# Pipelined routing head: one tile between producer and consumer, scatters in pairs, a shorter sort before the last slots

## The chip, the core and the metric

The kernel runs on one core of a Trainium2 chip, as one launch. The metric is the device time of a run in microseconds (us); lower is better. Before the change the median of three runs is 5019.25 us (5018.96 to 5019.48). The core's engines run beside each other, each through its own queue in order: TensorE (PE, with its weight loads shown apart as PEld), VectorE (DVE), ScalarE (ACT), GpSimd (POOL), and SyncE (SP), which here only issues DMAs.

## The reference

The program is one "macaron" block on x of shape (8, 1024, 512), that is, 8192 tokens of 512 numbers: half a feed-forward, attention, half a feed-forward.

```python
x = x + 0.5 * ffn(layernorm(x))
x = x + attention(layernorm(x))
x = x + 0.5 * ffn(layernorm(x))
```

The feed-forward is a mixture of 32 experts with one expert per token and a capacity of C = 320 tokens per expert:

```python
logits = xt @ w_router                      # 8192 x 32
probs = softmax(logits); top1 = argmax(probs); gate = probs[top1]
pos = cumsum(onehot(top1), axis=0)[token, top1] - 1
accepted = pos < C
slot = where(accepted, top1 * C + pos, E * C)
buf[slot] = xt                              # E x C x 512
y = (silu(buf @ w_gate) * (buf @ w_up)) @ w_down
out = xt + where(accepted, y[slot] * gate, 0)
```

So the place of a token among those of its expert depends on all tokens before it. The attention has 16 heads of 32, with rotary embedding, and doesn't change here.

## The kernel before

Each feed-forward has two stages. A **head** finds the expert, the gate and the slot of every token and scatters (token number, gate) into a table in DRAM, one row of 8 bytes per token. The **experts' stage** (`experts`, L443) reads this table back, gathers the tokens of one expert after another from DRAM by index, computes, and scatters the results.

In the first half of the program the head is `front` (L287). Its loop (L343) goes over 64 tiles of 128 tokens. The tiles form nine groups: 4 tiles, seven times 8, and 4. In iteration i it

- normalizes tile i on ACT (`h`, L134), transposes it on PE in four matmuls (`tp`, L156), and copies the transposed tile i - 1 from PSUM to SBUF (`xT`, L355; on ACT, every eighth on DVE),
- takes the mean and variance of tile i + 10 on DVE (`stats`, L113 and L114),
- moves every open piece of work one step on (`advance`). Such a piece is a Python generator: each `yield` in it ends its step for this iteration; what the `yield` says (WAIT, PE, DVE) is not used in this loop.

Three kinds of generators are open. `normalizing` (L116) makes the scales of a group: a sum on DVE (L124), a power on POOL (`rstd`, L125), and one step later their products on DVE (`nmr`, L127). `routers` (L176) makes the logits of four tiles: eight passes of PE for `pl` (L184), a copy on ACT (`parts`, L189), a step later eight for `lp` (L194) and a copy on ACT (`lg`, L197). `route` (L200) takes a whole group: maxima on DVE, an exponential on ACT (L227), one-hot columns and their running counts (`oh`, `run`, L232 to L238), PE products that count the tokens before each one (`pp`, L242 and L246), the position (L250 to L258), then 14 small DVE operations that turn it into the slot, and at last the group's scatters, one per tile, all in one step, as indirect DMAs of POOL (L279). A group's `route` begins only when that of the group before has ended, since the running counts go on from it.

The order on PE, ACT, DVE and POOL is the order of these Python calls (`manual_schedule`). Only SP's order is left to the compiler of the program. So an instruction that waits holds up all that is behind it on its engine.

When the loop and its open work are done, `sorted` (L373) ranks the experts by their token counts. It gives a matrix that puts the table's columns in this order, `order` (which expert is first, read by SP to find its weights) and `arm` (which of three copies of the experts' loop fits the counts). In it some 36 DVE operations and four matmul pairs depend on each other.

`experts` then loads the table (`slots`, L478), folds its last columns (L483), multiplies it by the matrix (`pt`, L486), turns the result into indices (`come`, L488), starts the gathers of the first two experts (L555), loads the first expert's weights with three DMAs of 1 MB (L546), and clears two buffers `a` on POOL (L482), which the experts' activations are written to.

In the second half of the program the head's work is spread through the attention (`finished`, L1276), group by group of four tiles, with its own scheduler (`step`, `product`); `sorted` follows after the last group (L885).

Of the kernel before, what the change touches and what calls it, by code (L numbers as in the profile page):

```python
# [14 lines left out]
I32 = mybir.dt.int32  # L15
# [35 lines left out]
class Block:  # L51
# [58 lines left out]

    def stats(self, pool, mv, x):
        st = pool.tile([P, 6], F32, tag="bnst", bufs=4, name="st")
        self.nc.vector.bn_stats(st, x)  # L113
        self.nc.vector.bn_aggr(mv, st)  # L114
# [61 lines left out]
    def routers(self, xT, lg, pool, psum, tag, bufs):  # L176
# [6 lines left out]
        for k in range(KD):  # L183
            nc.tensor.matmul(  # L184
                pl[k * E : (k + 1) * E, :], self.w_router[:, k, :], xT[:, k, :],
                start=True, stop=True,
            )
        parts = pool.tile([P, 4 * P], F32, tag="parts", bufs=bufs, name="parts")
# [4 lines left out]
        for j in range(4):  # L193
            nc.tensor.matmul(  # L194
                lp[:, j, :], parts[:, j * P : (j + 1) * P], self.fold, start=True, stop=True
            )
        self.copy(lg, lp)  # L197
        yield WAIT, 1

    def route(self, t0, lg, pool, psum, tag, carry, table, spare=None):  # L200
# [8 lines left out]
        def wide(name):  # L209
            return pool.tile([P, G, E], F32, tag=name, bufs=1, name=name)  # L210
# [26 lines left out]
        for j in range(G):  # L237
            nc.vector.tensor_tensor(run[:, j + 1, :], run[:, j, :], oh[:, j, :], ALU.add)  # L238
        yield WAIT, 1
# [9 lines left out]
        )  # L249
        nc.vector.tensor_tensor(lg, pp, oh, ALU.mult)  # L250
# [5 lines left out]
        pos, ok, s, u = narrow("pos"), narrow("ok"), narrow("s"), narrow("u")  # L256
        slot = narrow("slot", I32)
        nc.vector.tensor_reduce(pos, lg, AX.X, ALU.add)  # L258
        yield DVE, 2.0

        nc.vector.scalar_tensor_tensor(s, m, float(-P), pos, ALU.mult, ALU.add)
        for i in range(1, self.NB):
            nc.vector.tensor_scalar(
                u, pos, float(i * P), float((E - 1) * P), ALU.is_ge, ALU.mult
            )
            nc.vector.tensor_tensor(s, s, u, ALU.add)

        nc.vector.tensor_scalar(ok, pos, float(C), None, ALU.is_lt)
        nc.vector.tensor_scalar(s, s, float(E * P - self.NS), None, ALU.add)
        nc.vector.tensor_tensor(s, s, token, ALU.subtract)  # L270
        nc.vector.tensor_tensor(s, s, ok, ALU.mult)
        nc.vector.tensor_tensor(s, s, token, ALU.add)
        nc.vector.tensor_scalar(slot, s, float(self.NS), None, ALU.add)
        if spare is not None:
            nc.vector.tensor_scalar(ok, pos, float(C), None, ALU.is_ge)
            nc.vector.scalar_tensor_tensor(u, token, float(-self.T), ok, ALU.add, ALU.mult)
            nc.vector.tensor_scalar(spare[:, t0 : t0 + G], u, float(self.T), None, ALU.add)
        for j in range(G):
            nc.gpsimd.indirect_dma_start(  # L279
# [7 lines left out]
    def front(self, pool, psum, x, rest, spare, carry, table):  # L287
# [12 lines left out]
        def load(t):  # L300
            xs[t // 4] = xq = pool.tile([P, 4, D], F32, tag="xq", bufs=6, name="xq")
# [13 lines left out]
        def routed(g):  # L315

            while state.next < g:
                yield
            state.carry = yield from self.route(
                starts[g], lgs[g], pool, psum, "lp", state.carry, table, spare  # L320
            )
            state.next += 1

        def products(t):
# [3 lines left out]
                xTs.pop(t // 4), lg[:, at : at + 4, :], pool, psum, "lp", bufs=2  # L328
# [11 lines left out]
        ahead, late = G + 2, None  # L340
        load(0)
        load(4)
        for i in range(-ahead, NT + 2):  # L343
            if 0 <= i < NT:
# [3 lines left out]
                h = pool.tile([P, D], F32, tag="h", bufs=4, name="h")  # L348
                self.normalize(h, tile_of(i), (r, n, None, None), i)
                if i % 4 == 0:  # L350
                    xTs[i // 4] = pool.tile([P, KD, 4 * P], F32, tag="xT", bufs=3, name="xT")
                tp = self.turned(psum, "tp", h)
            if late:
                to, from_, j = late
                (nc.vector.tensor_copy if j % G == G - 1 else nc.scalar.copy)(to, from_)  # L355
                if j % 4 == 3:
                    work.append(products(j))
            late = None
            if 0 <= i < NT:
                late = xTs[i // 4][:, :, i % 4 * P : (i % 4 + 1) * P], tp, i  # L360
# [10 lines left out]
        return state.carry  # L371

    def sorted(self, pool, psum, tag, counts):  # L373
# [3 lines left out]
        nc, E, NB = self.nc, self.E, self.NB  # L377
        R = NB * E
        wide = pool.tile([P, NB, E], F32, name="wide")
        for i in range(NB):  # L380
            nc.vector.tensor_copy(wide[:, i, :], counts)


        keys, mine = pool.tile([P, E], F32, name="keys"), pool.tile([R, E], F32, name="mine")
        many = pool.tile([R, P], F32, name="many")
        pc = psum.tile([P, E], F32, tag=tag, name="pc")
        nc.tensor.matmul(pc, self.ones, counts, start=True, stop=True)
        nc.vector.scalar_tensor_tensor(keys, pc, float(E), self.rev[:, 0, :], ALU.mult, ALU.add)
        pr = psum.tile([R, P], F32, tag=tag, name="pr")
        nc.tensor.matmul(  # L390
            pr, wide.rearrange("p b e -> p (b e)"), self.ones, start=True, stop=True
        )
        nc.vector.tensor_copy(many, pr)
        nc.vector.tensor_scalar(mine, many[:, 0:E], float(E), None, ALU.mult)
        nc.vector.tensor_tensor(mine, mine, self.rev[:R, 0, :], ALU.add)

        own = pool.tile([R, E], F32, name="own")
        for i in range(NB):
            at = slice(i * E, (i + 1) * E)
            nc.vector.tensor_copy(own[at, :], self.ident[at, at])  # L400
        key, rank = pool.tile([R, 1], F32, name="key"), pool.tile([R, 1], F32, name="rank")
        nc.vector.tensor_tensor(mine, mine, own, ALU.mult)
        nc.vector.tensor_reduce(key, mine, AX.X, ALU.add)
        nc.vector.tensor_scalar(mine, keys[:R, :], key, None, ALU.is_gt)
        nc.vector.tensor_reduce(rank, mine, AX.X, ALU.add)

        place = pool.tile([R, E], F32, name="place")
        nc.vector.tensor_scalar(place, self.rev[:R, 0, :], -1.0, float(E), ALU.mult, ALU.add)
        nc.vector.tensor_scalar(place, place, rank, None, ALU.is_equal)
        matrix = pool.tile([R, R], F32, name="matrix")  # L410
        nc.vector.memset(matrix, 0.0)
        for i in range(NB):
            at = slice(i * E, (i + 1) * E)
            nc.vector.tensor_copy(matrix[at, at], place[at, :])

        cols = pool.tile([E, 2, P], F32, name="cols")
        nc.vector.tensor_tensor(mine[0:E, :], self.rev[0:E, 0, :], self.ident[0:E, 0:E], ALU.mult)
        nc.vector.tensor_reduce(rank[0:E, :], mine[0:E, :], AX.X, ALU.add)
        nc.vector.tensor_scalar(rank[0:E, :], rank[0:E, :], -1.0, float(E), ALU.mult, ALU.add)
        nc.vector.tensor_copy(cols[:, 0, :], rank[0:E, :].to_broadcast([E, P]))  # L420
# [996 lines left out]
```

## Time and profile before

| what | value |
|---|---|
| median of the runs | 5019.25 us |
| profiled execution: its own time | 5020.19 us |
| profiled execution: span from first to last instruction | 5018.3 us |
| PE busy | 4682.0 us (93% of the span) |
| DVE busy | 2869.2 us (57%) |
| ACT busy | 2927.2 us (58%) |
| POOL busy | 790.2 us (16%) |
| mean granted PE clock | 0.962 |

Busy time by stretch, in us, with the granted clock of PE as a share of full speed:

| stretch (us) | PE | DVE | ACT | POOL | PE clock |
|---|---|---|---|---|---|
| 80 to 120 | 19.53 | 15.56 | 13.16 | 16.86 | 0.59 |
| 120 to 160 | 22.18 | 21.52 | 15.69 | 9.43 | 0.54 |
| 200 to 240 | 16.71 | 18.57 | 9.52 | 22.37 | 0.63 |
| 240 to 280 | 12.36 | 17.37 | 2.98 | 12.68 | 0.51 |
| 300 to 320 | 20.00 | 7.93 | 3.54 | 6.80 | 1.00 |

The first experts' stage begins its matmuls at 274.57 us and ends near 1085, the attention lasts to about 4160, and the second experts' stage begins its matmuls at 4196.53.

How to read it: a row of the timeline or of a group names the line, the engine, the operation and, as out<-in, the tiles; in brackets stand the idle time before it and what ended that. In the chain of waits each row is a start in us, a length in us, and the engine, tile and line that carried the time. A row of waits gives who waited for whom: us in total, times, and the longest. A PE that is busy at half clock does half the work, so the clock stands beside it.

### The profile page before, as it was taken

What the parts mean: (1) busy time and instruction counts of PE and PEld (TensorE: products, weight loads), DVE (VectorE), ACT (ScalarE), POOL (GpSimd) and SP (SyncE); (2) the same over time, 40 slices, a digit from 0 to 9 for tenths busy, and PEclk for the clock granted to TensorE, in tenths of its full rate; (3) what the DMA queues carried; (4) which work ended last, traced back from release to release, by engine and by line L of the source; (5) the groups of instructions that cost most, each with busy time, mean ns of one, the idle gap of its engine ahead of it and who ended that gap; (6) DMA issues with size and microseconds to landing.
All of it is one profiled execution on the core that took longest, in us unless ns stands there. A gap on an engine that the chain in (4) does not pass through costs nothing.

```text
span 5018.3 us, 68972 instructions
## 1 busy us (share of the span) xinstructions
PE 4682.0 (93%) x24572; PEld 2150.1 (43%) x24572; DVE 2869.2 (57%) x5678; ACT 2927.2 (58%) x5851; POOL 790.2 (16%) x773
## 2 busy tenths in 40 slices
PE   5489999978899999999999999999999876999998
PEld 3256666753223333333333333333333224666676
DVE  5433333335766777777777777777777744333332
ACT  4311112115998888888888888888888841111111
POOL 2322333211000000100010110110110002222221
PEclk6689999988999999999999999999999997999999
DMA  3055556641111211221211212212211124445553
GB/s 128 10 200 179 183 185 197 207 158 32 35 34 34 72 58 48 71 57 53 71 54 54 72 46 64 66 45 66 60 41 56 47 68 153 157 163 168 165 186 132
DMA packets 290538, 486.07 MB, mean 97 GB/s; under 512 B 47847, under 2 KB 83121, under 8 KB 290176
## 3 DMA queue, kind: packets, MB, share of 16 engines
q1 hardware_dynamic: 255328, 404.36, 25.6%
q0 software_dynamic: 34560, 76.93, 5.0%
q8 instruction: 197, 3.23, 0.3%
q14 instruction: 165, 1.35, 0.1%
q10 hardware_dynamic: 288, 0.20, 0.0%
HBM read 380.11 MB, written 89.72 MB: 94 GB/s over the span
## 4 chain that ended last, share of the span: by engine, by line
PE 80%; DVE 8%; ACT 5%; issue 3%; POOL 1%; DMA 1%; SPq 1%; DVEq 0%; POOLq 0%; ACTq 0%
PE sa L1153 13%; PE gp L638 9%; PE up L638 9%; PE pq L1058 8%; PE yp L677 8%; PE po L1235 8%; PE sb L1133 5%; PE px L1261 4%; PE pv L1103 4%; PE sb L1160 3%; ACT junk L1172 2%; DVE nm L1168 2%; PE tp L156 2%; PE tp L626 2%; PE yp L685 1%
## 5 line engine op out<-in xcount | busy, mean ns | idle before, releaser
L1168 DVE TENSOR_REDUCE nm<-sa 128x2 f32<-128x1024 f32 x1024 | 1249.4, 1221 | 650.3 <-PE sa L1153 388.0
L1172 ACT ACTIVATE junk<-sa,nm 128x512 f32<-128x512 f32 x2048 | 1408.2, 688 | 268.1 <-DVE nm L1168 194.5
L1153 PE MATMUL sa<-k,q 32*128 32x512 f32 x4096 | 1149.8, 645 | 20.9 <-ACT junk L1172 11.4
L1165 ACT ACTIVATE pr<-sb 128x1024 f32<-128x1024 f32 x1024 | 1041.3, 1018 | 99.3 <-PE sb L1160 95.0
L1160 PE MATMUL sb<-q,k 32*128 32x512 f32 x4096 | 1062.7, 602 | 0.0
L643 ACT ACTIVATE sg<-gp 128x320 f32<-128x320 f32 (+3 forms) x256 | 102.9, 402 | 1229.0 <-PE gp L638 1092.9
L1083 POOL TENSOR_TENSOR raw<-raw,cs 128x512 f32<-128x512 f32 x128 | 165.1, 1289 | 2474.5 <-DMA rot<-raw 1746.0
L1235 PE MATMUL po<-pr,v 128*32 128x512 f32 x4096 | 548.8, 607 | 0.1
L638 PE MATMUL gp<-bT,wg 128*128 128x320 f32 (+3 forms) x2048 | 533.3, 404 | 2.8 <-issue 2.0
L638 PE MATMUL up<-bT,wu 128*128 128x320 f32 (+3 forms) x2048 | 525.1, 399 | 0.0
L1058 PE MATMUL pq<-hT,wqk 128*128 128x512 f32 x1024 | 510.6, 623 | 6.6 <-DVE raw L1073 3.6
L677 PE MATMUL yp<-wd,a 128*128 128x512 f32 x1024 | 453.7, 596 | 0.0
L638 PEld LDWEIGHTS gp<-bT,wg 128*128 128x128 f32 x2048 | 387.8, 191 | 118.9 <-issue 31.6
L1133 PE MATMUL sb<-mrow,ones 3*128 3x512 bf16 x2048 | 393.4, 385 | 43.6 <-ACT pr L1165 38.9
L638 PEld LDWEIGHTS up<-bT,wu 128*128 128x128 f32 x2048 | 389.5, 190 | 94.7 <-issue 0.8
L662 DVE TENSOR_TENSOR a<-sg,up 128x320 f32<-128x320 f32 (+3 forms) x256 | 114.2, 446 | 550.7 <-PE up L638 510.5
L1133 PEld LDWEIGHTS <-ones 3*128 3x128 bf16 x2048 | 100.6, 91 | 711.9 <-issue 670.5
L1172 ACT ACTIVATION_READ_ACCUMULATOR junk<-sa,nm 128x1 f32 x2048 | 397.8, 194 | 0.0
L1160 PEld LDWEIGHTS sb<-q,k 32*128 32x128 f32 x4096 | 360.0, 184 | 0.1
L1153 PEld LDWEIGHTS sa<-k,q 32*128 32x128 f32 x4096 | 305.2, 184 | 86.2 <-ACT pr L1165 36.0
L1058 PEld LDWEIGHTS pq<-hT,wqk 128*128 128x128 f32 x1024 | 176.1, 191 | 325.3 <-issue 227.4
L681 DVE SCALAR_TENSOR_TENSOR ys<-yp,at,x 128x512 f32<-128x512 f32 x128 | 96.1, 751 | 369.0 <-PE yp L677 369.0
(179 smaller groups left out, 4341.0 us busy)
## 6 DMA issues: line engine op xcount, KB each, us to landing
wg<-in_w_gate SPq DMA_DIRECT2D x64, 1024.0 KB
wu<-in_w_up SPq DMA_DIRECT2D x64, 1024.0 KB
wd<-in_w_down SPq DMA_DIRECT2D x64, 1024.0 KB
rot<-raw SPq DMA_DIRECT2D x1024, 32.0 KB
xq<-in_x SPq DMA_DIRECT2D x16, 1024.0 KB
all<-in_x SPq DMA_DIRECT2D x32, 512.0 KB
xt<-first_rows SPq DMA_DIRECT2D x64, 256.0 KB
xr<-first_rows SPq DMA_DIRECT2D x64, 256.0 KB
```

The costliest lines, as they stand in the source:

```text
L638: nc.tensor.matmul(acc, w[:, k, f * P : (f + 1) * P], to.bT[:, k, 0:width], start=(k == 0), stop=(k == s.KD - 1),)
L677: nc.tensor.matmul(yp, a[:, f, i * P : (i + 1) * P], wd[:, f, :], start=(f == 0), stop=(f == KF - 1),)
L1058: nc.tensor.matmul(acc, w[:, which, k, :], self.hT[b, n][:, k, :], start=(k == 0), stop=(k == KD - 1),)
L1103: nc.tensor.matmul(acc, hT[:, k, at : at + P], self.w_vo[:, k, :], start=(k == 0), stop=(k == KD - 1),)
L1133: nc.tensor.matmul(sb[:, h, :], self.ones16[at : at + 3, :], row[at : at + 3, :], start=True, stop=False,)
L1153: nc.tensor.matmul(sa[:, h, :], qa[at, (g * 4 + j) * P : (g * 4 + j + 1) * P], ka[at, m * 512 : (m + 1) * 512], start=True, stop=True,)
L1160: nc.tensor.matmul(sb[:, h, :], k[at, t * P : (t + 1) * P], q[at, n * 512 : (n + 1) * 512], start=False, stop=True,)
L1165: nc.scalar.activation(pr, sb, AF.Exp)
L1168: nc.vector.tensor_reduce(nm[:, m, j, pair : pair + 2], sa, AX.X, ALU.max, negate=True)
L1172: nc.scalar.activation(self.junk, sa[:, h - pair, :], AF.Exp, bias=nm[:, m, j, h : h + 1], accum_out=se[:, m, j, h : h + 1],)
L1235: nc.tensor.matmul(self.po[at : at + HD, :], self.v[b][t][:, c * P + at : c * P + at + HD], prs[h // 2 * 2][:, h % 2, :], start=(t == 0), ...
L1261: nc.tensor.matmul(acc, self.oT[b, c, half][:, j * P : (j + 1) * P], self.w_vo[:, c, :], start=False, stop=(c == KD - 1),)
```

## The change

It has six parts.

1. In `front` the h of a tile is made two iterations ahead of its transposition, the statistics 12 iterations ahead instead of 10, and the copy of the transposed tile is issued ahead of the next transposition. A seventh buffer `xq` is there for the rows.
2. With `apart`, `routers` and `route` end their step between a PE product and the copy or product that reads it from PSUM. The scatters of a group are issued two in a step. A group's `route` may begin its counts as soon as the group before has its own (`counted`).
3. The slots take 9 DVE operations instead of 14, from three constants made at the start (`past`, `away`, `beyond`).
4. `sorted` takes the counts as soon as the last group has them. Six DVE operations make the matrix from constants; `rest` makes `order` and `arm` on one partition instead of 128. `route` runs it ahead of the last group's slots.
5. In `experts` the first expert's weights are issued on SP ahead of the table's load, and `come` is made straight from PSUM.
6. The buffers `a` are made and cleared once, at the start; the attention keeps its cosines and sines in them.

The diff, cut to its core:

```diff
 def constants(self, pool, w_router):
...
+        for t, add in (
+            (self.past, NS), (self.away, NS - E * P), (self.beyond, -self.T)
+        ):
+            nc.vector.tensor_scalar(t, self.token, float(add), None, ALU.add)
...
+        nc.gpsimd.memset(self.columns, -1.0)
+        for i in range(NB):
+            at = slice(i * E, (i + 1) * E)
+            nc.vector.tensor_copy(self.own[at, :], self.ident[at, at])
+            nc.vector.tensor_scalar(
+                self.columns[at, at], self.rev[at, 0, :], -1.0, float(E), ALU.mult, ALU.add
+            )
...
+        self.acts = [pool.tile([P, self.KF, self.C], F32, name=f"a{i}") for i in range(2)]
+        for t in self.acts:
+            nc.gpsimd.memset(t, 0.0)

 def routers(self, xT, lg, pool, psum, tag, bufs, apart=False):
...
+        if apart:
+            yield WAIT, 1
         parts = pool.tile([P, 4 * P], F32, tag="parts", bufs=bufs, name="parts")
         self.copy(parts, pl)
...
+        if apart:
+            yield WAIT, 1
         self.copy(lg, lp)

 def route(..., spare=None, apart=False, counted=None):
...
+        order = counted and counted(run[:, G, :])
         yield WAIT, 1
         yield PE, 1.2
         pp = psum.tile([P, G, E], F32, tag=tag, name="pp")
...
+        if apart:
+            yield WAIT, 1
         nc.vector.tensor_tensor(lg, pp, oh, ALU.mult)
...
+        if order:
+            at_once(order)
+
+        tokens = slice(t0, t0 + G)
+        nc.vector.tensor_scalar(u, pos, float(P), None, ALU.is_ge)
+        for i in range(2, self.NB):
+            nc.vector.scalar_tensor_tensor(u, pos, float(i * P), u, ALU.is_ge, ALU.add)
         nc.vector.scalar_tensor_tensor(s, m, float(-P), pos, ALU.mult, ALU.add)
+        nc.vector.scalar_tensor_tensor(s, u, float((E - 1) * P), s, ALU.mult, ALU.add)
+
+        nc.vector.tensor_tensor(s, s, self.away[:, tokens], ALU.subtract)
+        nc.vector.scalar_tensor_tensor(s, pos, float(C), s, ALU.is_lt, ALU.mult)
+        nc.vector.tensor_tensor(slot, s, self.past[:, tokens], ALU.add)
...
         for j in range(G):
+            if apart and j % 2 == 0:
+                yield WAIT, 1
             nc.gpsimd.indirect_dma_start(

 def front(...):
-            xs[t // 4] = xq = pool.tile([P, 4, D], F32, tag="xq", bufs=6, name="xq")
+            xs[t // 4] = xq = pool.tile([P, 4, D], F32, tag="xq", bufs=7, name="xq")
...
+            def counted(counts):
+                state.carry = counts
+                state.next += 1
+                if state.next == len(sizes):
+                    return ranked(counts)
...
-        ahead, late = G + 2, None
+        ahead, soon, late, hs = G + 4, 2, None, {}
...
         for i in range(-ahead, NT + 2):
+            if 0 <= (t := i + soon) < NT:
+                hs[t] = pool.tile([P, D], F32, tag="h", bufs=soon + 2, name="h")
+                self.normalize(hs[t], tile_of(t), (r, n, None, None), t)
+            if late:
+                to, from_, t = late
+                (nc.vector.tensor_copy if t % G == G - 1 else nc.scalar.copy)(to, from_)
+                if t % 4 == 3:
+                    work.append(products(t))

 def sorted(self, pool, psum, tag, counts):
...
         nc.tensor.matmul(pc, self.ones, counts, start=True, stop=True)
+        nc.vector.scalar_tensor_tensor(
+            keys, pc[:R, :], float(E), self.rev[:R, 0, :], ALU.mult, ALU.add
+        )
+        nc.vector.tensor_tensor(mine, keys, self.own, ALU.mult)
         nc.vector.tensor_reduce(key, mine, AX.X, ALU.add)
+        nc.vector.tensor_scalar(mine, keys, key, None, ALU.is_gt)
         nc.vector.tensor_reduce(rank, mine, AX.X, ALU.add)
+        nc.vector.tensor_scalar(matrix, self.columns, rank, None, ALU.is_equal)
+
+        def rest():
...
+            nc.vector.tensor_copy(order, pq[:, 0, :])
+            for j in range(n):
+                nc.vector.tensor_tensor(over[:, j, :], pq[:, 1, :], self.most[:, j, :], ALU.is_gt)
+            nc.vector.tensor_reduce(some, over, AX.X, ALU.max)
+            nc.vector.tensor_reduce(both, some, AX.X, ALU.add)
+            nc.vector.tensor_copy(arm, both)

 def experts(...):
-            acts = [tp.tile([P, self.KF, self.C], F32, name=f"a{i}") for i in range(2)]
+            acts = self.acts
...
+                expert = Expert(self, (tp, tp, ps), src, views, come, go, gates, acts)
+                first = load(expert, 0)
                 rows = fp.tile([R, P, 2], F32, name="slots")
                 nc.sync.dma_start(
                     rows, table[0 : self.NS, :].rearrange("(r s) c -> r s c", s=P)
                 )
-                for t in acts:
-                    nc.gpsimd.memset(t, 0.0)
...
+                    if i == 0:
+                        nc.vector.tensor_scalar(come, pt, float(T - 1), None, ALU.min)
                     nc.vector.tensor_copy(at[i], pt)
-                nc.vector.tensor_scalar(come, ids, float(T - 1), None, ALU.min)
...
-                states[0].weights = load(expert, 0)
+                states[0].weights = first

 class Attention:
-                self.start(self.finished(b, 1))
+                self.start(self.finished(b, 1, self.ranked))
                 self.finish()
-                self.ranks = self.s.sorted(self.ranking, psum, "m", self.carry)
...
-        self.cs = wp.tile([P, L], F32, name="cs")
-        self.sn = wp.tile([P, L], F32, name="sn")
+        self.cs, self.sn = (a.rearrange("p k c -> p (k c)")[:, 0:L] for a in s.acts)
```

## The prediction

> **What bounds the kernel now.** I read the page's slices, then the chain that ended last inside one turn of the head's loop, then the waits by engine, then the timeline at the end of both heads.
>
> ```profile
> PE 5489999978899999999999999999999876999998
> PEclk6689999988999999999999999999999997999999
> ```
>
> A slice is 125 us. In most of the span PE is 90% busy at full clock; in the first two slices it is half busy at 0.6. The head's loop and its end, up to the first gather of the experts at 255.61, stand there. The chain of one turn (eight tiles, 87.54 to 117.57):
>
> ```profile
> 107.49 0.18 DVE u L276
> 107.67 1.03 POOL table L279
> ...
> 116.60 0.96 POOL table L279
> 117.57 1.68 POOL rstd L125
> 119.28 0.17 DVE nmr L127
> ```
>
> and the waits of 60 to 215 us:
>
> ```profile
> POOL table L279 <- DVE u L276: 81.2, 5, 18.5
> PE tp L156 <- ACT h L134: 66.8, 33, 9.1
> DVE nmr L127 <- POOL rstd L125: 44.1, 6, 9.6
> ACT parts L189 <- PE pl L184: 34.9, 11, 4.2
> ```
>
> No engine is full; they take turns. POOL runs eight scatters (0.96 + 0.30 us each) and only then the pow for the next scales, so DVE stands 9.6 us in each turn. In the other 20 us ACT copies what PE has just made and PE transposes what ACT has just made, within one tile. A turn takes 29.4 us (pow at 58.18, 87.54, 117.57, 147.62, 176.69). The end of the head, first half then second half of the program:
>
> ```profile
> 241.47 0.96 POOL L279 DMA_INDIRECT table<-row,slot  x1 [0.31 <-issue]
> 244.40 2.27 POOL L482 MEMSET a<- 128x1280 f32 x2 [1.96 <-remote]
> 245.54 0.35 SPq L478 DMA_DIRECT2D slots<-table  x1
> 251.89 0.41 SPq L546 DMA_DIRECT2D wg<-in_w_gate  x1
> 255.61 0.98 POOL L555 DMA_INDIRECT x<-in_x,come  x1 [8.94 <-DVE come L488]
> ```
> ```profile
> 4171.04 0.96 POOL L279 DMA_INDIRECT table<-row,slot  x1 [0.30 <-issue]
> 4174.02 0.33 SPq L478 DMA_DIRECT2D slots<-table  x1
> 4174.28 2.27 POOL L482 MEMSET a<- 128x1280 f32 x2 [2.28 <-DVE over L433]
> 4175.10 0.41 SPq L546 DMA_DIRECT2D wg<-in_w_gate  x1
> 4178.77 0.99 POOL L555 DMA_INDIRECT x<-x,come  x1 [2.21 <-DVE come L488]
> ```
>
> From the end of the last scatter to the first gather it is 13.2 us in the first head (the sort runs to 252.9) and 6.8 us in the second, where the sort hides beside the scatters and their landing. In both, what first touches the memory of the experts' stage (the memset, the slot table's load) comes 2 to 3 us after the last scatter's end: the stage waits for the landing.
>
> **The change, part by part.**
>
> *The loop.* Cost of a turn by engine, from the spacing of starts in dense stretches of the timeline. DVE: eight stats at 0.82 = 6.6; maxima to the product with rev 1.7; indices and running counts 2.7; the position product 0.3; sums and rows 1.25; slots 2.25 for 14 operations now, 9 afterwards, about 1.45; one xT copy 0.6; scales 0.4. Sum 15.0. ACT: eight h at 0.72, seven xT copies at 0.48, two parts, two lg, one exp: 10.9. POOL: 8 x 1.26 + 1.68 = 11.8; with DVE busy (195.8 to 199.7) scatters took 1.03 to 1.17, so up to 13. PE at half clock: eight transposed tiles at 1.11, pl 2 x 1.9, lp 2 x 1.56, pp 1.7: 17.5; at full clock, from its rows at 103 and 135 us (0.66, 1.04, 0.98), 10.2.
> In the new order every such result has an iteration before its use, h has two, and the scatters of a group fall into four iterations. Counted from the yields, the pow comes in the fourth of these, ahead of its two scatters: behind six. Their 7.6 us lie beside DVE work of 7.7 us (stats, maxima, indices, stats); then 1.7 us of pow stand against 1.4 us of DVE. The wait of 9.6 falls to 0.3 to 1.2; I take 0.8. A turn is then 15.8 by DVE if PE keeps up.
> *The clock decides whether it does.* Row first: in 3 us slices, PE busy 2.99 of 3.00 at 99 to 102 is followed by a granted clock of 1.00 in the next slice; and the clock fell to 0.53 at 30 to 33 after slices with 2.55 and 1.50 busy and no gap over 1.5 us. The Trainium skill, "TensorE: Matmul & The Clock Gate", Part 1, has it that the clock drops only after a whole idle window of 3.4 us; by that the new loop, without such gaps, stays at full clock and PE needs 10.2 per turn. By the row it need not stay up; held at half for good, PE would set 17.5. But a PE that lags is fully busy, which lifts it. I take 16.0 to 16.5 per turn.
> *Loop end T.* By DVE: first stats at 7.4; its work up to the loop's end (64 stats, 5.5 full routes, a part of the seventh group's, scales, copies, 1.5 of new constants at the start) is 109; pow waits 8 x 0.8 = 6; the last twelve tiles have no stats, ACT and PE set them, +9. T = 131. By PE with 16: 13.1 + 128 - 5 for what lags behind the loop = 136. I take 134; ends 118 (nothing waits) and 153 (PE at half clock). Before, the last xT copy is at 214.4, so T was 215.
> *The drain.* With the later steps three groups (8, 8, 4 scatters) are left for it. Rows of DVE: slots of the first at T + 3.2, scatters to T + 13.4; maxima, indices, the last group's too, and the sort's six operations (0.18 to 0.25) put the second group's slots at T + 17.3; eight scatters to 27.5, the last four to T + 32.6, their slots being ready by T + 22. Before: 242.4 - 215 = 27.4. So 5 us are given back. Last scatter ends at 166.6 instead of 242.4: **-75.8**.
> *After the last scatter.* The sort is gone from here. But expert 0's weights now go ahead of the slot table on SP. They fill memory of the stage that waits for the landing, so they can't start earlier although the order is known: three loads 0.59 apart from S + 2.3 (S the scatter's end), then the table, behind 3 MB on SP's queue. At the 390 GB/s of 247 to 275 us that is 8.1 us. Row for a small load behind large ones: the 2 KB bias loads (issued 1090.0 to 1091.4, behind 1 MB of tables) were waited for until 1094.57, where the slot table alone took 1.9. The Trainium skill, "DMA: Bandwidth & Descriptors", Queues, rings and completion order, agrees that each DMA engine consumes a ring in order, and speaks against this edit. Table landed at S + 12.7, fold copy, matmul and index 2.5 (from the second head): gather at S + 15.2, against 13.2 and 6.8 now: +2.0 and +8.4. If the table were not held up: -6.6 and -0.2. I take the first, as the row is direct. What comes back: gathered rows now land 6.9 and 6.7 us after the first issue, beside that same 3 MB; without it 0 to 4 less; I take 2 each: **-4**.
> *Second head otherwise.* The sort's first half stands ahead of the position product: its count matmul and six DVE operations put it 1.5 us later; the rest (six small operations, 1.2) stands ahead of the slots, which are 0.6 shorter. Last scatter +2.1.
> *At nothing:* eight small constants on POOL and the memsets of the two buffers (2.3 us) lie before POOL's first pow at 10.97, where it idles from 2.4; their removal at 244 was off the path. cos and sin in those buffers: loads at 1089.14 stand behind the experts' last PE reader (1085) already. A seventh xq buffer: DMA had the rows in time.
>
> **Sum.** -75.8 + 2.0 + 8.4 - 4 + 2.1 = -67.3. The profiled execution took 5020.2 (span 5018.3): 4952.9; the median of the runs is 0.9 lower: **4952**. Own range 4934 to 4970 (T from 118 to 150).
>
> **The rivals.**
> - *The table isn't held up* (weights start early, or its packets pass): both heads 8.4 better: 4935. For: order is known some 10 us before S. Against: both first touches above. 17%.
> - *PE stays at half clock*: T = 153, 4971. For: nearly every slice of 87 to 150 shows 0.50. Against: the slice after full busyness. 15%.
> - *The stall only moves*: DVE still waits some 5 us per turn for the pow, since POOL slows beside a busy DVE; T about 170, 4988. 4%.
> - *Slower*: the 3 MB ahead of the slot table. Price 2 x 8.4 = 16.8, with the drain's 5.2 and the second head's 2.1 some 24 us. It decides once the loop gains less, that is with T over 190, a turn over 23 us: the loop would have to keep most of its waits, that is, the change not do what it says. About 5030. 4%.
>
> **Chances.** Forecast 60%. A difference of 0.2% (10 us) is about what a measurement can tell from no change. All cases but the last are faster: 0.95; same 0.02; slower 0.03. Range 4926 to 4982: it holds the forecast, most of the first two rivals, and some 10 us for waits without a releaser, as at 239 to 244 now.
>
> **What would show it.** Turns of 15.5 to 17 us between pows, the wait of nmr for rstd under 1.5 each; granted clock of the head's loop 0.55 to 0.8; the last scatter of the first head near 167; wg issued 2 to 3 us after it and the slot table after wd; first gather some 15 us after the last scatter in both heads, near 182 in the first. Wrong if the table lands within 4 us, if DVE idles over 3 us per turn, or if anything after the experts' first matmuls changes length.

## The result and the profile after

| | before | after | ratio |
|---|---|---|---|
| first session, median | 5019.36 us | 4952.53 us (4950.23 to 4954.77) | 0.9866 [0.9849, 0.9883] |
| first session, span of the profiled execution | 5018.3 us | 4951.4 us | |
| later sessions, median | 5009.8 us | 4935.43 us (4933.82 to 4938.60) | 0.9849 [0.9832, 0.9865] |
| later sessions, span of the profiled execution | 5009.6 us | 4936.8 us | |

In brackets behind a ratio stands its 95% interval. The forecast was 4952. The total came out; the way to it did not in every step. The later sessions, whose kernels are the experiments below, ran the old kernel some 10 us and the changed one some 17 us faster than the first. The first experiment shows where most of that lay, though not its cause. The first session is therefore compared with itself alone. In each of the three later ones the old kernel ran too and took 5009.4 to 5009.8 us, so their runs are compared with one another.

The slices of the changed kernel's page, 124 us each:

```profile
PE   6499999969899999999999999999999876999998
PEclk8699999979999999999999999999999988999999
```

The first two slices, half busy at 0.6 before, are still the poor ones; the second is now the end of the head, not its loop. The waits from 38 to 137 us (who waited for whom: us in total, times, longest):

```profile
POOL table L331 <- DVE spare L327: 14.8, 4, 5.7
...
PE tp L194 <- ACT h L172: 11.1, 6, 5.6
...
ACT lg L240 <- issue: 6.1, 1, 6.1
...
ACT xT L408 <- remote: 4.6, 1, 4.6
ACT parts L230 <- remote: 3.0, 1, 3.0
...
DVE nmr L165 <- POOL rstd L163: 1.9, 5, 0.4
```

The wait for the power (`rstd`) has gone from 9.6 us a turn to at most 0.4. These powers start at 38.77, 53.58, 68.90, 84.22 and 99.71: a turn takes 14.8 to 15.5 us, where it took 29.4. What is new are three waits of ScalarE whose end the profile puts down to nothing in the program ("issue", "remote"). The timeline of ScalarE (start, duration, operation, idle before it):

```profile
114.53 0.59 ACT L408 COPY xT<-tp 128x512 f32<-128x512 f32 x1
121.19 0.27 ACT L240 COPY lg<-lp 128x128 f32<-128x128 f32 x1 [6.07 <-issue]
121.36 0.81 ACT L172 ACTIVATE h<-xq,nmr,rstd 128x512 f32<-128x512 f32 x1
126.80 0.59 ACT L408 COPY xT<-tp 128x512 f32<-128x512 f32 x1 [4.63 <-remote]
130.42 0.59 ACT L230 COPY parts<-pl 128x512 f32<-128x512 f32 x1 [3.04 <-remote]
```

The product lp that the first of these copies reads was made on PE at 113.11 to 114.1. Up to 115 us the loop was some 12 us ahead of the forecast (without the standstill it ends at 121.6, as the next section shows). Here it lost all of that: the last xT copy ended at 137.5 (forecast 134). The end of the first head:

```profile
169.06 0.96 POOL L331 DMA_INDIRECT table<-row,slot  x1 [0.31 <-issue]
171.73 0.39 SPq L578 DMA_DIRECT2D wg<-in_w_gate  x1
...
172.90 0.37 SPq L578 DMA_DIRECT2D wd<-in_w_down  x1
173.32 0.63 SPq L513 DMA_DIRECT2D slots<-table  x1
183.25 0.22 DVE L516 COPY slots<-slots 32x128 f32<-32x128 f32 x1 [24.52 <-DMA slots<-table]
...
185.72 0.99 POOL L587 DMA_INDIRECT x<-in_x,come  x1 [15.69 <-DVE go L526]
```

The weights go out 1.7 us after the last scatter, the table's load last, and its use waits until 9.9 us after the issue: it did stand behind the 3 MB, as forecast.

### The profile page after: what moved, and what is told of

Read it like the earlier page. It is cut to its first block, busy times and chain, and to the rows that moved or that the text cites. A ratio compares the mean times of both kernels' runs of the same rounds, so it can differ in the third digit from the quotient of the medians.

```text
span 4951.4 us, 68819 instructions
## 1 busy us (share of the span) xinstructions
PE 4649.6 (94%) x24568; PEld 2134.3 (43%) x24568; DVE 2842.6 (57%) x5530; ACT 2923.9 (59%) x5851; POOL 789.8 (16%) x779
## 4 chain that ended last, share of the span: by engine, by line
PE 81%; DVE 8%; ACT 4%; issue 3%; DMA 2%; POOL 1%; SPq 1%; another core or an unknown queue 0%; DVEq 0%; POOLq 0%; ACTq 0%
PE sa L1184 13%; PE gp L670 10%; PE up L670 9%; PE pq L1089 9%; PE po L1266 9%; PE yp L709 8%; PE sb L1164 5%; PE px L1292 4%; PE pv L1134 4%; PE sb L1191 3%; ACT junk L1203 2%; DVE nm L1199 2%; PE tp L658 2%; PE tp L194 2%; PE yp L717 1%
## 5 line engine op out<-in xcount | busy, mean ns | idle before, releaser
L1114 POOL TENSOR_TENSOR raw<-raw,a 128x512 f32<-128x512 f32 x128 | 165.0, 1289 | 2400.8 <-DMA rot<-raw 1638.9
L694 DVE TENSOR_TENSOR a<-sg,up 128x320 f32<-128x320 f32 (+3 forms) x256 | 114.1, 446 | 554.1 <-PE up L670 515.0
```

## The experiments

Twelve runs were made: both kernels once more, and ten variants. Four expectations (old_slots_in_attention, table_ahead_of_weights, scatters_at_once, no_tile_between) name times at the level of the first session; they are read as differences from the changed kernel. Each run has one profile, and that of the changed kernel fell on the slowest of its four executions (4938.60, median 4935.43), so a few us between two medians need not show in their profiles.

**The changed and the old kernel once more.**

> The changed kernel once more, unchanged, beside the others. My theory: what stood from 116 to 137 us of its first profile (ScalarE without an instruction for 6.1, 4.6 and 3.0 us) is not of the kernel, since two experiments whose first head is the same to the instruction did not show it: the last xT copy then comes near 122.3 and the last scatter ends near 155.2, and the ratio to the kernel before is 0.984 to 0.985 where the kernel before takes 5010. Rival: it comes back in the same place, with the last scatter near 170 and a ratio of 0.9866.

> The kernel before, unchanged, for its profile beside the others. My theory: like the changed kernel it runs here without the stall that its first profile shows (239 to 244 us), so its sort lies beside the last scatters and the first gather comes 6.6 us after the last scatter instead of 13.2, near 250; from the first to the last oT it takes 2803 to 2806 us, since the restored planner cost was worth 5 to 6 us of the 11 and the rest was between executions. Rival: the attention takes 2808.5 us again, then the planner's number alone accounts for 9 us.

The changed kernel took 4935.43 us, the old one 5011.39 in its one run. The same stretch of ScalarE in the changed kernel's second profile:

```profile
114.57 0.59 ACT L408 COPY xT<-tp 128x512 f32<-128x512 f32 x1
115.04 0.29 ACT L240 COPY lg<-lp 128x128 f32<-128x128 f32 x1
...
115.91 0.60 ACT L408 COPY xT<-tp 128x512 f32<-128x512 f32 x1
116.38 0.62 ACT L230 COPY parts<-pl 128x512 f32<-128x512 f32 x1
```

Up to 115 us the two profiles agree to 0.1 us; then the same three copies that stood 13.7 us in the first follow each other at once. The last xT copy ends at 121.6 and the last scatter at 153.69, instead of 137.5 and 170.02. In the old kernel's second profile, the sort's PE products:

```profile
235.68 0.71 PE L390 MATMUL pr<-ones,wide 128*96 128x128 f32 x2 [4.12 <-DVE keys L388]
240.77 1.03 PE L426 MATMUL pq<-place,cols 32*128 32x32 f32 x4 [4.38 <-DVE cols L421]
```

In its first profile pr came at 243.53 after 12.69 us of "remote". So the old sort does hide beside the scatters: the first gather comes at 249.71, 6.6 us after the last scatter (243.13) and not 13.2. Both expectations hold here; from the first to the last oT the old kernel took 2806.2 us, just past the range. What stood the engines still in the first session is not of the kernel alone: the same program ran without it. In both first profiles there is a stretch in which only POOL's scatters ran (116.6 to 121.2 us here, 239.3 to 242.4 in the old kernel). No instruction packet is recorded between 114.6 and 149 us of the changed kernel's, so a late fetch doesn't show there. The later sessions ran on two chips; which one the first ran on is not on record. The cause stays open.

**Where the attention's 10 us come from.** The first comparison held an effect that the forecast put at nothing. From the first to the last of the 64 tiles oT, which take the attention's output, it took 2808.5 us before and 2797.5 after.

```diff
 # old_slots_in_attention: in route, where not apart
+            nc.vector.tensor_scalar(u, pos, float(i * P), float((E - 1) * P), ALU.is_ge, ALU.mult)
...     # the old 11 operations in place of the 7
```

> The slots of the second head, whose groups of four tiles lie in the attention, are made with the old 11 operations instead of 7; the first head keeps the new ones. My theory: the 10 us that the changed kernel gains between the first oT of the attention and the last one come from these four operations in each of 15 or 16 groups, since VectorE is dense there; so the run is 8 to 12 us slower than the changed kernel, 4961 to 4965, with the experts' first matmul still near 209. Rival: the gain there has another source (the cosines' new place, another interleaving), then within 3 us of 4952.5.

4939.28 us, 3.9 over the changed kernel. The attention took 2795.5 us against 2795.8, and the profiled span is even 1.2 shorter (4935.6 against 4936.8), so the profiles don't show the 3.9 us. The theory fell: here the four operations cost next to nothing. The next suspect was the order on VectorE. The second head's planner reads what a yield names as the cost of its step, and with the shorter slots the change had lowered one such number, from 2.0 to 1.5 (a line of the diff that the cut one above doesn't show).

```diff
 # planner_cost_restored: the changed kernel
-        yield DVE, 1.5
+        yield DVE, 2.0
 # before_planner_cost: the kernel before
-        yield DVE, 2.0
+        yield DVE, 1.5
```

> Only the cost that the step ahead of the slots names to the second head's planner goes back from 1.5 to 2.0; the short slots stay. The first head does not use the number. My theory, formed after the old slots cost nothing in the attention: with 2.0 the planner puts the slots' step behind another reduction nm, as before, and that order costs; from the first to the last oT it takes 2804 to 2809 us as in the kernel before instead of 2797, and the run is 7 to 12 us slower than the changed kernel. Rival: the order is worth nothing and the gain is of the short slots or of the cosines' place after all: within 3 us of the changed kernel.

> The kernel before, with that one number at 1.5 instead of 2.0 and nothing else. My theory: the attention's first to last oT takes 2795 to 2799 us instead of 2808.5, and the run is 8 to 12 us faster than the kernel before, a ratio of 0.9976 to 0.9984. Rival: the number alone does nothing (ratio 0.9995 to 1.0005).

| first to last oT, us | number 2.0 | number 1.5 |
|---|---|---|
| 11 operations | 2806.2 (before) | 2799.4 (before_planner_cost), 2795.5 (old_slots_in_attention) |
| 7 operations | 2799.2 (planner_cost_restored) | 2795.8 (changed) |

The cell with two kernels differs by 3.9 us, although both have the same operations and the same number; and kernels with the changed one's attention lie between 2792.4 and 2795.8. So this measure is too coarse. A narrower one is steady: from the slots of the first of the 16 groups to those of the eleventh it takes 1810.8 to 1812.5 us in all eight such kernels of the later sessions.

| slots of group 1 to slots of group 11, us | number 2.0 | number 1.5 |
|---|---|---|
| 11 operations | 1819.7 (before) | 1813.3 (before_planner_cost), 1813.1 (old_slots_in_attention) |
| 7 operations | 1817.5 (planner_cost_restored) | 1812.2 (changed) |

In time, the number alone made the old kernel 5004.35 us, a ratio of 0.9987 [0.9979, 0.9994], and its return cost the changed kernel 6.4 us (4941.85). Both signs were right, both sizes below what was expected (7 to 12 and 8 to 12), and with the number restored the attention did not go all the way back to 2804. In the narrow measure the number is worth 6.4 us with the old operations and 5.3 with the new, close to the 5.5 and 6.4 in time. The short slots are worth 0.9 to 2.2. The two together make 7.5 of the 10.4 us; the other 2.9 lie outside these groups and were not traced. VectorE in the old kernel's second profile:

```profile
2083.41 1.21 DVE L1168 TENSOR_REDUCE nm<-sa 128x2 f32<-128x1024 f32 x1
2085.21 0.75 DVE L1073 TENSOR_SCALAR raw<-pq,bias 128x512 f32<-128x512 f32 x1 [0.59 <-PE pq L1058]
2086.28 1.23 DVE L1168 TENSOR_REDUCE nm<-sa 128x2 f32<-128x1024 f32 x1 [0.32 <-PE sa L1153]
2087.97 0.69 DVE L160 COPY hT<-tp 128x512 f32<-128x512 f32 x1 [0.46 <-PE tp L156]
...
2094.08 1.20 DVE L266 TENSOR_TENSOR s<-s,u 128x4 f32<-128x4 f32 x1
...
2096.10 0.17 DVE L273 TENSOR_SCALAR slot<-s 128x4 int32<-128x4 f32 x1
2096.18 1.22 DVE L1168 TENSOR_REDUCE nm<-sa 128x2 f32<-128x1024 f32 x1
```

and with the number at 1.5:

```profile
2082.79 1.21 DVE L1168 TENSOR_REDUCE nm<-sa 128x2 f32<-128x1024 f32 x1
2083.92 0.15 DVE L261 SCALAR_TENSOR_TENSOR s<-m,pos 128x4 f32<-128x4 f32 x1
...
2085.58 0.17 DVE L273 TENSOR_SCALAR slot<-s 128x4 int32<-128x4 f32 x1
2085.66 0.74 DVE L1073 TENSOR_SCALAR raw<-pq,bias 128x512 f32<-128x512 f32 x1
2086.32 1.22 DVE L1168 TENSOR_REDUCE nm<-sa 128x2 f32<-128x1024 f32 x1
```

In the first VectorE waits for PE three times (0.59, 0.32, 0.46), and later runs the slots where it is the one that is late: the next nm stands behind them. In the second the same operations lie in that gap, and the three rows after them start without a wait. With 2.0 the slots come so late in every second group up to the tenth, five in all, with 1.5 in none; the same holds for the changed kernel with either number. Part of the price is stranger: in three of the five late groups one small operation lasts 0.5 to 1.3 us instead of 0.2 (L266 above), in all some 2.5 us. Its cause isn't known.

**The other suspect, the cosines' place.** It had been a rival from the first.

```diff
-            acts = self.acts
+            acts = [tp.tile([P, self.KF, self.C], F32, name=f"a{i}") for i in range(2)]
...
-        self.cs, self.sn = (a.rearrange("p k c -> p (k c)")[:, 0:L] for a in s.acts)
+        self.cs = wp.tile([P, L], F32, name="cs")
```

> The buffers a are made and cleared in the experts' stage again, after the slot table's load is issued, and the attention keeps its cosines and sines in tiles of its own; all else as changed. My theory: the clearing lies beside the table's 13 us, the loads of the cosines behind the experts' last work: within 3 us of 4935.4, the attention's first to last oT at 2794 to 2798. Rival: the place of the cosines is what shortened the attention: 2799 us or more there and 4 to 7 us slower.

4934.70 us, the attention 2795.4 us. The place of the cosines is worth nothing, as forecast.

**The slot table ahead of the weights.**

```diff
-                first = load(expert, 0)
                 rows = fp.tile([R, P, 2], F32, name="slots")
                 nc.sync.dma_start(rows, table[0 : self.NS, :]...)
+                first = load(expert, 0)
...     # and SP's order in this stage by hand
```

Since SP's order is otherwise the compiler's, it was set by hand in this stage. The loads behind these follow in the same order in both profiles (second expert, `all`, third expert).

> The slot table's load is issued ahead of the first expert's three weight loads in both heads; all else as changed. My theory: the table no longer waits behind 3 MB; it lands some 8 us earlier in each head, the first gather is 6.5 to 7.5 us after the last scatter instead of 15.7, the rows then land 6.7 to 7.6 us after their gather as before, and the run gains 14 to 18 us: 4935 to 4939. Rival one: gathered rows and first matmul then wait for the weights' 3 MB, so that half is given back: about 4944. Rival two: the table's load is late for another reason (the scatters' landing), then within 2 us of 4952.5.

4914.99 us, 20.4 under the changed kernel, a ratio of 0.9806 [0.9790, 0.9822].

```profile
154.20 0.96 POOL L331 DMA_INDIRECT table<-row,slot  x1 [0.30 <-issue]
156.81 0.35 SPq L512 DMA_DIRECT2D slots<-table  x1
157.93 0.41 SPq L578 DMA_DIRECT2D wg<-in_w_gate  x1
...
158.84 0.22 DVE L516 COPY slots<-slots 32x128 f32<-32x128 f32 x1 [14.95 <-DMA slots<-table]
...
161.31 0.99 POOL L587 DMA_INDIRECT x<-in_x,come  x1 [6.15 <-DVE go L526]
...
167.54 0.69 DVE L151 BATCH_NORM_STATS2 st<-x 128x6 f32<-128x512 f32 x1 [6.23 <-DMA x<-in_x,come]
```

The table is used 2.0 us after its issue, where it took 9.9. The first gather comes 6.15 us after the last scatter instead of 15.64, in the second head 6.28 (from 4069.78 to 4076.06) instead of 16.29. And the rows land 6.2 us after their gather, where they took 7.3, although the first expert's 3 MB are under way then. 9.5 + 1.1 in the first head and 10.0 + 1.2 in the second are 21.8; 20.4 arrive. The mechanism of the theory holds. The gain is above its 14 to 18, since the gather came a little earlier and the rows landed sooner than expected. Both rivals fell.

**The parts of the loop, one at a time and together.**

```diff
 # scatters_at_once
-            if apart and j % 2 == 0:
+            if apart and j == 0:
 # no_tile_between: routers with apart=False, and in route
-        if apart:
-            yield WAIT, 1
         nc.vector.tensor_tensor(lg, pp, oh, ALU.mult)
 # h_not_ahead
-        ahead, soon, late, hs = G + 4, 2, None, {}
+        ahead, soon, late, hs = G + 4, 0, None, {}
 # loop_parts_undone: all three
```

> All scatters of a group in one step, as before, instead of two in a step; all else as changed. My theory: the power stands behind eight scatters again, VectorE waits 2.5 to 4.5 us for it in each of six turns, a turn takes 18 to 20 us instead of 15.4, the run is 10 to 25 us slower than the changed kernel: 4962 to 4977. Rival: since the scatters begin earlier in the turn the power is only just later, and the loop's end, which stalls from 115 to 137 us anyway, hides it: within 4 us of 4952.5.

> The tile between a PE product and the copy or product that reads it is taken out in the routers and the route; h two tiles ahead and scatters in pairs stay. My theory: ScalarE's copies and VectorE's position product wait for PE within one tile again, at half clock 1 to 2 us each for two parts, two lg and one pp a turn, so a turn of 17 to 20 us: 10 to 25 us slower than the changed kernel, 4962 to 4977. Rival: h ahead and the copy ahead of the transposition already cover these waits: within 4 us of 4952.5.

> h of a tile is made in the iteration of its transposition again instead of two before; all else as changed. My theory: PE waits for ScalarE in each tile, a turn takes 17 to 20 us instead of 15.4, the run is 10 to 25 us slower: 4945 to 4960. Rival: the copy ahead of the transposition is enough cover: within 4 us of 4935.4.

> h not ahead, no tile between PE and its readers, and all scatters of a group at once: three of the loop's parts undone together; statistics 12 tiles ahead, the copy ahead of the transposition, the counts handed on early, the short slots and the sort stay. My theory: the waits of the kernel before come back for the most part, a turn of 21 to 26 us, 35 to 65 us slower than the changed kernel: 4970 to 5000. Rival: the parts that stay hold most of the gain: a turn under 19 us and under 4960.

| | time, us | turns, us | last scatter's end |
|---|---|---|---|
| before | 5009.8 | 29 to 30 | 243.13 |
| loop_parts_undone | 4984.29 | 20.4 to 22.1 | 203.89 |
| scatters_at_once | 4942.12 | 17.4 to 17.6 | 161.94 |
| changed | 4935.43 | 14.8 to 15.5 | 153.69 |
| h_not_ahead | 4933.01 | 14.8 to 15.5 | 158.24 |
| no_tile_between | 4930.68 | 14.5 to 15.0 | 153.10 |

With all scatters at once VectorE waits for the power again, in three turns:

```profile
DVE nmr L165 <- POOL rstd L163: 7.4, 3, 2.5
```

The place was right, the price smaller than expected: 6.7 us in time where 10 to 25 were. The theory of the missing tile fell, its turn did not grow. Its loop ends 5.1 us later (126.70 against 121.61), but the last scatter ends where that of the changed kernel does. It is 4.8 us faster in time, more than its rival allowed; the attention, whose code is the same, is 3.0 shorter in this profile (2792.8), so the gain isn't put down to the tile. The theory of h fell too, and its rival holds in time: the turn is the same, and the cost is 4.6 us at the last scatter. In time even that is lost in another difference, told below. But the three together are worth 49 us, as expected. These are the waits with all three undone (60 to 115 us):

```profile
POOL rstd L163 <- DVE rstd L162: 23.7, 3, 11.4
PE tp L194 <- ACT h L172: 17.2, 17, 1.4
DVE lg L298 <- PE pp L294: 16.3, 3, 5.8
ACT parts L230 <- PE pl L223: 14.3, 5, 3.7
ACT lg L240 <- PE lp L235: 10.9, 5, 2.6
```

Two of these come back with one part alone, and the turn isn't longer for it: PE waits 15.9 us for h in h_not_ahead, and ScalarE 12.7 us for pl in no_tile_between. What needs the three together are VectorE's wait for pp (16.3 us, at most 1.5 in each of the three alone), ScalarE's for lp and POOL's for the sum of VectorE. VectorE sets the turn of the changed kernel, so a wait that doesn't reach it is free. That is how the parts seem to cover for one another; no two of them were undone as a pair. And here POOL waits for VectorE's sum, not the other way round: the 9.6 us for the power are gone without the pairs. They went with what stays in this kernel (statistics 12 tiles ahead, counts handed on early, the copy ahead of the transposition, short slots, the sort); which of these did it was not tried apart.

**The best version.**

> The changed kernel with the slot table's load ahead of the first expert's weights, and without the tile between PE and its readers. My theory: the table's 17 us and whatever the missing tile is worth add up: 15 to 19 us under the changed kernel, within 3 us of the kernel with the table ahead alone. Rival: the missing tile is itself worth some 10 us, then 24 to 30 us under the changed kernel.

4913.73 us, a ratio of 0.9804 [0.9787, 0.9820]: within 1.3 us of the table ahead alone, as expected. Both beat the changed kernel by over 20 us, where 15 to 19 were expected.

## Why the prediction came out, step by step

Differences after minus before, in us; "later" sets the second profiles of both kernels against each other. The rows are rounded.

| step | forecast | first session | later |
|---|---|---|---|
| last scatter of the first head | -75.8 | -72.4 | -89.4 |
| from there to the first gather | +2.0 | +2.5 | +9.1 |
| gather to the first row statistics | -2 | +0.6 | +0.4 |
| these to the experts' first matmul | 0 | +4.1 | +3.7 |
| first matmul to the second head's last `run` | 0 | -13.2 | -9.7 |
| that `run` to its last scatter | +2.1 | +1.8 | +1.8 |
| last scatter to gather | +8.4 | +9.1 | +9.5 |
| gather to first statistics | -2 | +0.9 | +1.1 |
| the rest | 0 | -0.3 | +0.8 |
| sum | -67.3 | -66.9 | -72.8 |

- **The loop and its turn: right in kind, too slow in size.** The wait of the power went, at 0.4 us where 0.8 was taken. VectorE sets the turn as summed (15.0 and the waits). The "+9" for the last twelve tiles and the wait in each turn were too much: undisturbed the loop ended at 121.6, near the lower end that was given (118), not 134. The forecast had 15 us for these two beside VectorE's 7.4 + 109; 5.2 remain. In the first session a standstill of 13.7 us that the forecast could not know filled the difference. That was luck. The drain of 32.6 measured 32.5 and 32.1.
- **The clock.** Between 40 and 114 us PE's longest wait for an engine is 1.7 us, yet the granted clock is 0.74 and 0.73 in the second profile's windows. The clock is granted in steps of 3.41 us, and cut at these steps the windows show when it falls (length; PE, PEld, DVE, ACT and POOL busy; clock, DMA share, GB/s):

```profile
60.00:80.00 20.00, 16.56 (x95) 10.83 (x94) 18.31 (x66) 13.94 (x27) 12.65 (x12) 0.74 0.45 106
80.00:100.00 20.00, 15.42 (x79) 10.01 (x80) 18.04 (x68) 15.00 (x28) 12.75 (x14) 0.73 0.03 2
```
```profile
62.06:65.47 3.41, 1.67 (x12) 0.84 (x8) 3.21 (x9) 2.03 (x5) 2.50 (x4) 1.00 0.88 267
65.47:68.88 3.41, 2.43 (x5) 1.43 (x6) 3.06 (x14) 3.29 (x6) 2.41 (x3) 0.50 0.14 42
...
109.84:113.25 3.41, 2.42 (x16) 1.68 (x14) 3.10 (x13) 3.41 (x7) 2.50 (x4) 1.00 0.02 1
113.25:116.66 3.41, 3.41 (x31) 2.41 (x30) 2.93 (x16) 3.41 (x8) 2.50 (x4) 1.00 0.03 5
```

  Between 40 and 127 us it falls five times, each time after a step in which PE was busy 1.1 to 1.7 us, with no pause over 1.7; after steps with 2.4 us or more it stays. So in this trace a step less than half busy lowers it, and PE need not be idle for a whole one. By the table in the Trainium skill ("TensorE: Matmul & The Clock Gate", Part 1), which lets the clock fall after an idle window of some 3.4 us, it should have stayed up; the same part also tells of a kernel whose short pauses between bursts made the clock swing, and that is nearer to these rows. The measurement decides: the range 0.55 to 0.8 holds, and it did not matter, since VectorE is at 18 of 20 us and PE at 15 to 17.
- **The table behind 3 MB: right**, in both heads, with 9.1 to 9.5 where the second head's +8.4 was taken. For the first head the forecast subtracted 13.2, a number of the old kernel's disturbed profile; against the undisturbed 6.6 it is +9.1. That one row of one execution can hold a standstill was seen ("waits without a releaser, as at 239 to 244 now") and put into the range, not into the step.
- **The rows' landing: wrong.** "without it 0 to 4 less; I take 2 each" gave -4; the two heads together measured +1.5, in either session. The 3 MB of the first expert were gone by then, but the second expert's follow once the table is in (168.56 us in the second profile, the gather at 169.33), then `all` and the third expert's, so the rows land beside other loads all the same. And in table_ahead_of_weights, where the first two experts' weights lie beside the gathers, they land sooner (6.2), while the DMAs move more: 389 GB/s from gather to landing against 324. So the load beside the rows did not set their landing in the way supposed; what did stays open.
- **Gather to matmul: missing.** PE stands before the experts' first matmul, at the entry of the chosen copy of their loop. The last bT copy ends at 187.13 in the changed kernel and at 191.95 with h not ahead, and then (second profile of the changed kernel, then h_not_ahead):

```profile
192.73 1.94 PE L670 MATMUL gp<-bT,wg 128*128 128x320 f32 x3 [6.13 <-DVE n L167]
```
```profile
192.20 2.47 PE L670 MATMUL gp<-bT,wg 128*128 128x320 f32 x4 [0.78 <-DMA wg<-in_w_gate]
```

  5.6 us against 0.25. VectorE's n, which the first row names, is not what the matmul needs: with h not ahead it started before that n was made. In the first a 16 KB packet of an instruction queue runs from 189.9 to 191.0, inside the wait; in the second the next one is at 194.9, after the matmul. The fourteen profiles of this case agree. In the first head of all but h_not_ahead such a packet ends 1.7 to 1.8 us ahead of the matmul. In the ten of the changed kernel and its variants the wait is 5.6 to 5.7. In the three of the old kernel and its variant the packet ends about when the last bT copy does, and the wait is 1.5 to 1.8. In all fourteen second heads the packet comes after the matmul, and the wait is 0.25. So the matmul follows the packet; why it comes late is not shown. The Trainium skill ("Runtime: NRT & Kernel Launch", Instruction fetch mechanics) says that a taken branch to a page that isn't loaded waits for its DMA; these rows fit that, but no run moved the branch or the code by itself.
- **The attention at nothing: wrong.** The forecast named the second half's steps for the sort alone and left out that the shorter slots, and the number that stands for their cost, also lie in 16 groups of the attention. It is the largest term put at nothing, -10.4 in the later profiles: 5.3 to 6.4 for the number, 0.9 to 2.2 for the slots, 2.9 not traced.
- **Two slips that changed nothing.** With the forecast's own terms (13.2 + 2.0 and 6.8 + 8.4, or 6.6 without a hold-up) the hold-up is worth 8.6 us a head, not 8.4. And the case "slower" sets in at T over 201, not 190: its 24 us take 8.4 for each head, where the sum has +2.0 for the first and -4 for the landings.

So the total of the first session was met to 0.4 us by luck, by errors that cancel: +3.4 at the last scatter (a loop 12 us faster than summed, less the standstill), +5.5 in the landings, +4.1 at the branch and +1.2 at the gathers, against -13.2 in the attention and its surroundings and -0.6 elsewhere. The rival "the table isn't held up" would have read 4935; it is what the experiment with the table ahead then built, with 20.4 where it had 16.8. (That the later sessions' median is 4935 too is chance: there the table was held up and the loop was faster.) Of the forecast's own signs of error, "anything after the experts' first matmuls changes length" came true.

## What to carry to other kernels

A DMA that is ready early is not thereby worth issuing early: if its memory comes free no sooner than the small load that everything waits for, it should stand behind that load. Before costing an edit in a shared helper, list every place that calls it, and every number in it that a planner reads: here one constant was worth 5.5 and 6.4 us in time. A step of which one profile shows a wait without a releaser should be read in a second profile before it enters a sum. And parts that pass for nothing when undone one by one can be worth 49 us together, so undo them together before calling any of them idle.

## What the runs showed of the hardware that was not expected

- In one session, and in no profile of the later ones, ScalarE stood 6.1, 4.6 and 3.0 us while POOL went on with its scatters, PE and VectorE behind it; the same program ran through there otherwise. In the old kernel PE stood so for 12.7 us beside the last scatters. The cause stays open.
- Gathered rows land 6.2 to 7.0 us after their gather where the first two experts' weights are issued just ahead of it (old kernel, table_ahead_of_weights), and 6.6 to 7.6 us in the changed kernel and its variants with the weights first, where the first expert's are already in: more load beside them was not slower.
- PE's clock fell to half after steps of 3.41 us in which PE was busy 1.1 to 1.7 us, with no pause over 1.7 us.
- The experts' first matmul came 1.7 to 1.8 us after the end of a 16 KB packet of an instruction queue in thirteen of fourteen first heads, after PE had stood 1.5 to 5.7 us. In the fourteenth the packet came later than the matmul, and PE did not stand.
